# One matmul for the rows of B and C of both scan directions

## The chip, the cores and the metric

The kernel runs on one core of a Trainium2 chip, as one launch. The metric is device time in microseconds; before the change the median of three runs is 13519.48 us (13518.94 to 13551.32). Everything is float32.

## The reference

Eight images of 64 channels and 64 x 64 pixels go through four layers: an attention over all pixels, a block of windowed attention with an MLP, a dynamic filter, and a selective-scan layer. Only the last one is touched. With `x_flat` the pixels row by row and `x_t` column by column, it scans each image along four directions: both orders forwards (k = 0 and 1), and both backwards (k = 2 and 3).

```python
x_hwwh = jnp.stack([x_flat, x_t], axis=1)
xs = jnp.concatenate([x_hwwh, jnp.flip(x_hwwh, axis=-1)], axis=1)
x_dbl = jnp.einsum('bkdl,kcd->bkcl', xs, xproj_w)
dts, Bs, Cs = jnp.split(x_dbl, [R, R + N], axis=2)
dts = jnp.einsum('bkrl,kdr->bkdl', dts, dtproj_w)
dts = jax.nn.softplus(dts + dtproj_b[None, :, :, None])
A = -jnp.exp(A_logs).reshape(K, DI, N)
out_y = _selective_scan(xs, dts, A, Bs, Cs, Ds.reshape(K, DI))
...
def step(h, inp):
    u_t, dt_t, B_t, C_t = inp
    h = h * jnp.exp(dt_t[..., None] * A) + dt_t[..., None] * B_t[:, :, None, :] * u_t[..., None]
    return (h, jnp.einsum('bkcn,bkn->bkc', h, C_t))
```

There are DI = 128 channels and N = 16 states; R = 4 is the rank of dt. For every pixel and direction, B and C are 16 numbers each, made from the 128 channels of x at that pixel with weights of the direction's own. Directions k and k + 2 read the same pixels with different weights.

## The kernel before

The images are taken in four pairs (p = 0 to 3). What a pair needs before its scans is `front`, what follows them is `back`. While pair p is scanned, `scans` runs `back(p - 1)` and `front(p + 1)` beside it: these are generators that yield costs, and after each scan step as many of their pieces are written as the share of steps done allows. The scans of the last pair have only `back(2)` beside them, and `back(3)` comes after.

A *unit* is one chunk of TD = 512 pixels of one image in one direction. A pair has 64 units, in the order of directions k = 1, 3, 0, 2 for each image (`nth` counts them), 8 chunks each; k = 1 and 0 take the chunks from 0 to 7, k = 3 and 2 from 7 to 0. In the whole kernel there are 256 units, which this document numbers from 0 to 255: units 0 to 7 are k = 1, 8 to 15 are k = 3, 16 to 23 are k = 0, 24 to 31 are k = 2, and so on; 64, 128 and 192 begin the next pairs.

`inputs` prepares a unit: it loads `xs` (L1697), makes dt from it (matmul `pdd` L1700, exp L1702 and ln L1705 on ACT, dt times x in `du` L1706 on DVE, a copy of dt in `du` L1707 on ACT), then the 32 rows of B and C (matmul `pbc` L1709, copy `bc` L1711 on ACT) and writes the rows to memory (`rows`, L1713). It is called after step 1 of the unit before.

A unit has 8 *steps*, of two states each. `fetch` (L1720) loads the two rows of B, or of C, from `rows` and spreads them over all 128 partitions, 512 KB each time; B three steps ahead and C two steps ahead of use, with three buffers each. `products` (L1725) multiplies B with dt times x on POOL, two steps ahead. `step` takes exp of dt times A on ACT into a PSUM bank (`dad`, L1747; three banks with the tag `da`, which `pdd` and `pbc` also use), scans on DVE (L1750), keeps the last value in `carry` (L1758, ACT), and multiplies with C on POOL or DVE (L1761, L1765, L1770). `sums` adds up the states with matmuls into `yd` (L1789), and after a unit's last step adds the result to `Y` on DVE. For k = 2, the last direction, the sum goes into the unit's `xs` (L1804) and from there to memory (`ys`, L1805). `xs` has two buffers, `du` two, `rows` two.

For k = 1 and k = 2, `xs` is needed until the end of its unit, so its buffer is free for the unit after next only then; for k = 3 and k = 0 it is free as soon as the inputs are made.

The order in which instructions stand on each engine is made by a scheduler when the program is built: it takes the ready instruction that was written first, with a timing model of its own, and so may pull later-written instructions forward while others wait. SP issues all loads and stores of the scans from one queue, in a fixed order; an issue that waits holds those behind it.

Of the kernel before, what the change touches and what calls it, by code (L numbers as in the profile page):

```python
# [9 lines left out]
F32 = mybir.dt.float32  # L10
AF = mybir.ActivationFunctionType
# [12 lines left out]
DI, NST, RNK, KDIR = 128, 16, 4, 4  # L24
TD = 512
NTD = L // TD
# [62 lines left out]
def _pack(w):  # L89
    items = []  # L90

    def put(name, a):
        a = np.asarray(a, np.float32)
        shape = a.shape
        flat = a.reshape(shape[0], -1)
        if shape[0] < P:
            flat = np.concatenate([flat, np.zeros((P - shape[0], flat.shape[1]), np.float32)], axis=0)
        items.append((name, shape, flat))
# [91 lines left out]
    put("cb", _col(f["conv_b"]))  # L190
    xp = f["xproj_w"]
    put("xpT", np.concatenate([xp[:, RNK:], xp[:, :RNK]], axis=1).transpose(2, 0, 1))
    put("xbc", xp[:, RNK:].transpose(2, 0, 1))
    put("xr", xp[:, :RNK].transpose(1, 0, 2))
    put("drT", f["dtproj_w"].transpose(2, 0, 1))
    put("alogs", f["A_logs"].reshape(KDIR, DI, NST).transpose(1, 0, 2))
# [961 lines left out]
class _Direct:  # L1158
# [498 lines left out]
    def scans(self, p, beside, cost):  # L1657

        self.units = []
        for im in range(2):
            out = self.memory("ys")
            self.kept["y", 2 * p + im] = out
            for nth, k in enumerate((1, 3, 0, 2)):
                order = range(NTD) if k < 2 else range(NTD - 1, -1, -1)
                self.units += [dict(image=2 * p + im, k=k, c=c, at=at, nth=nth, out=out) for at, c in enumerate(order)]
        self.inputs(self.units[0])
        n = 8 * len(self.units)
        steps = [{} for _ in range(n)]  # L1670
        done = 0
        for i in range(-3, n):
            if i + 3 < n:
                self.fetch(i + 3, steps[i + 3], 0)
            if 0 <= i + 2 < n:
                self.fetch(i + 2, steps[i + 2], 1)
                self.products(i + 2, steps[i + 2])
            if i >= 0:
                self.step(i, steps[i])
                if i:  # L1680
                    self.sums(i - 1, steps[i - 1], steps[i]["w"])
                if p == B // 2 - 1 and done >= cost:
                    self.turn = max(self.turn, 0)
                while done < cost * (i + 1) / (n - LEAD):
                    done += next(beside, cost)
            if i % 8 == 1 and i // 8 + 1 < len(self.units):
                self.inputs(self.units[i // 8 + 1])
        self.sums(n - 1, steps[n - 1])
        self.run(beside)

    def inputs(self, u):

        nc, w, net = self.nc, self.w, self.net
        wk, ps = self.sw, self.ps
        k, c = u["k"], u["c"]
        x = u["x"] = wk.tile([P, TD], F32, name="xs", tag="xs")
        nc.sync.dma_start(x, self.kept[u["image"]][k % 2][:, c * TD : (c + 1) * TD])  # L1697

        pd = ps.tile([P, TD], F32, name="pdd", tag="da")
        nc.tensor.matmul(pd, lhsT=net.xdt[:, k, :], rhs=x, start=True, stop=True)  # L1700
        du = u["du"] = wk.tile([P, 2, TD], F32, name="du", tag="du")
        nc.scalar.activation(  # L1702
            pd, pd, AF.Exp, bias=w["dtb"][:, k : k + 1], accum_out=net.esum[:, u["image"], k, c : c + 1]
        )
        nc.scalar.activation(pd, pd, AF.Ln, bias=1.0)  # L1705
        nc.vector.tensor_tensor(du[:, 1], pd, x, ALU.mult)  # L1706
        nc.scalar.activation(du[:, 0], pd, AF.Copy)  # L1707
        pb = ps.tile([2 * NST, TD], F32, name="pbc", tag="da")
        nc.tensor.matmul(pb, lhsT=w["xbc"][:, k, :], rhs=x, start=True, stop=True)  # L1709
        bc = wk.tile([2 * NST, TD], F32, name="bc", tag="bc")  # L1710
        nc.scalar.activation(bc, pb, AF.Copy)  # L1711
        rows = u["rows"] = self.dram.tile([2 * NST, TD], F32, name="rows", tag="rows")
        nc.sync.dma_start(rows, bc)  # L1713

    def fetch(self, i, st, s):

# [245 lines left out]
```

## Time and profile before

| What | Value |
|---|---|
| median of 3 runs | 13519.48 us |
| the profiled execution | 13549.57 us |
| its span | 13547.6 us |
| mean granted TensorE clock | 0.882 |
| copy `bc` (L1711, ACT), 256 | median 586 ns |
| matmul `pbc` (L1709), 512 instructions for 256 | median 617 ns |
| weight load `pbc` (L1709), 512 | median 109 ns |
| matmul `pdd` (L1700), 512 instructions for 256 | median 668 ns |
| exp, ln, copy of dt (L1702, L1705, L1707; ACT) | median 662, 582, 577 ns |
| dt times x (L1706, DVE) | median 690 ns |
| product with B (L1725, POOL), 2048 | mean 2367 ns |
| scan (L1750, DVE) | mean 1270 ns |
| `B<-rows`, `C<-rows`, issue to landing | median 5.2, 4.6 us |
| `xs<-xt`, `xs<-xc`, issue to landing | median 3.5, 4.2 us |

A float32 matmul shows as two instructions. Durations of matmuls are modelled and overlap their neighbours, so what one takes of the engine is less than its duration when they follow each other closely. In the lines of waits the time is that in which the named engine, or SP's queue, stood before this line; what it stood for is the operation that came last. In timelines the columns are start, length (us), engine, line, operation, what it writes and reads, and the number merged.

### The profile page before, as it was taken

How to read it: one execution, taken by the hardware profiler on the slowest of the kernel's cores; microseconds unless marked ns; L12 is line 12 of the kernel's file. 1: busy time of each engine (PE TensorE's matmuls, PEld its weight loads, DVE VectorE, ACT ScalarE, POOL GpSimd, SP SyncE). 2: the span in 40 equal slices, each digit the busy share in tenths (PEclk: the TensorE clock that was granted, in tenths of full speed). 3: DMA queues.
4: the chain of work that ended last, by engine and by line, in shares of the span. 5: the costliest groups of instructions: out<-in, count | busy, mean ns of one | idle time of the engine just before them, and what ended most of it. 6: DMA issues, size and time to landing. Idle time of an engine off the chain costs nothing. (4 is left out here: it accounts for less than half of the span.)

```text
span 13547.6 us, 140341 instructions
## 1 busy us (share of the span) xinstructions
PE 10802.4 (80%) x45762; PEld 3981.2 (29%) x45762; DVE 8783.4 (65%) x10407; ACT 7087.6 (52%) x15569; POOL 7764.9 (57%) x3875
## 2 busy tenths in 40 slices
PE   9999986888787669989888667997898666666665
PEld 2243322333232222224432222223443222222221
DVE  0121236776668676676666767667675768988985
ACT  5556514564545646655554545665653644544542
POOL 0000004887778764466666685446675687777881
PEclk9999977998898779999889788998888788888887
DMA  0000004776667765455555674455554677787882
GB/s 24 1 1 1 3 13 170 238 238 211 207 218 244 235 200 168 155 186 175 169 178 175 221 250 168 158 167 176 186 192 151 209 241 262 235 280 264 303 283 86
DMA packets 706249, 2385.12 MB, mean 176 GB/s; under 512 B 81120, under 2 KB 81248, under 8 KB 704480
## 3 DMA queue, kind: packets, MB, share of 16 engines
q1 hardware_dynamic: 681312, 2319.76, 50.9%
q10 hardware_dynamic: 24192, 56.29, 1.1%
q8 instruction: 362, 5.93, 0.2%
q14 instruction: 383, 3.14, 0.1%
HBM read 2272.97 MB, written 102.76 MB: 175 GB/s over the span
## 5 line engine op out<-in xcount | busy, mean ns | idle before, releaser
L1725 POOL TENSOR_TENSOR vd<-B,du 128x1024 f32<-128x1024 f32 x2048 | 4832.8, 2367 | 3924.8 <-DMA B<-rows 2573.0
L1789 PE MATMUL yd<-vd,pack 128*128 128x512 f32 x7540 | 4263.8, 696 | 1381.0 <-POOL vd L1761 591.9
L1747 ACT ACTIVATE dad<-du,As 128x512 f32<-128x512 f32 x4096 | 2729.0, 681 | 1130.8 <-DVE hd L1750 684.1
L1750 DVE TENSOR_TENSOR_SCAN hd<-dad,carry,vd 128x512 f32<-128x512 f32 x2166 | 2713.2, 1270 | 677.8 <-ACT dad L1747 385.9
L1789 PEld LDWEIGHTS yd<-vd,pack 128*128 128x128 f32 x7540 | 1497.0, 215 | 3843.5 <-issue 1654.4
L1761 POOL TENSOR_TENSOR vd<-hd,C 128x1024 f32<-128x1024 f32 x658 | 1551.4, 2358 | 1068.2 <-DVE hd L1750 702.0
L1750 DVE TENSOR_TENSOR_SCAN dad<-dad,carry,vd 128x512 f32<-128x512 f32 x1418 | 1793.3, 1274 | 160.3 <-POOL vd L1725 99.1
L1765 POOL TENSOR_TENSOR vd<-hd,C 128x512 f32<-128x512 f32 x1154 | 1476.1, 1280 | 512.5 <-DVE hd L1750 446.4
L1313 ACT ACTIVATE e<-s 128x512 f32<-128x512 f32 x2048 | 1200.7, 591 | 751.1 <-PE s L1307 749.6
L1307 PE MATMUL s<-X 64*128 64x512 f32 x4096 | 1344.4, 646 | 30.5 <-ACT e L1313 28.8
L1299 PE MATMUL po<-e,VT 128*64 128x512 f32 x4096 | 1226.7, 621 | 12.6 <-ACT e L1313 9.9
L1765 DVE TENSOR_TENSOR vd<-dad,C 128x512 f32<-128x512 f32 x1300 | 864.9, 672 | 48.2 <-ACT carry L1758 39.1
L1758 ACT ACTIVATE carry<-hd 128x1 f32<-128x1 f32 (+1 forms) x1586 | 317.3, 201 | 920.3 <-DVE hd L1750 917.0
L1758 ACT ACTIVATE carry<-dad 128x1 f32<-128x1 f32 x1422 | 240.9, 169 | 804.1 <-DVE dad L1750 801.4
L1307 PEld LDWEIGHTS s<-X 64*128 64x128 f32 x4096 | 375.9, 186 | 915.2 <-issue 783.1
L1447 DVE TENSOR_TENSOR w_e<-w_s,bias 128x512 f32<-128x512 f32 x512 | 329.9, 681 | 424.3 <-PE w_s L1435 423.6
L1462 PEld LDWEIGHTS w_av<-vals,w_e 64*64 64x64 f32 x16384 | 546.7, 144 | 197.3 <-issue 86.8
L1462 PE MATMUL w_av<-vals,w_e 64*64 64x9 f32 x16384 | 574.9, 207 | 30.4 <-ACT w_e L1452 30.1
L1700 PE MATMUL pdd<-xs,xdt 128*128 128x512 f32 x512 | 348.3, 768 | 257.8 <-DMA xs<-xc 121.4
L1452 ACT ACTIVATE w_e<-w_e 128x512 f32<-128x512 f32 x512 | 311.8, 626 | 366.9 <-DVE w_e L1447 251.6
L1299 PEld LDWEIGHTS po<-e,VT 128*64 128x64 f32 x4096 | 236.1, 135 | 847.5 <-issue 763.9
L1574 PE MATMUL acc<-tap,pack 128*128 128x512 f32 x576 | 367.5, 761 | 99.5 <-DVE tap L1573 98.1
(252 smaller groups left out, 11129.2 us busy)
## 6 DMA issues: line engine op xcount, KB each, us to landing
B<-rows SPq DMA_DIRECT2D x2048, 512.0 KB, 5.2
C<-rows SPq DMA_DIRECT2D x2048, 512.0 KB, 4.6
xs<-xt SPq DMA_DIRECT2D x128, 256.0 KB, 3.5
xs<-xc SPq DMA_DIRECT2D x128, 256.0 KB, 4.2
xc<-xcv ACTq DMA_DIRECT2D x64, 256.0 KB, 4.0
zs<-z ACTq DMA_DIRECT2D x64, 256.0 KB, 3.7
xt<-XT ACTq DMA_DIRECT2D x32, 512.0 KB, 7.8
rows<-bc SPq DMA_DIRECT2D x256, 64.0 KB, 1.6
```

What stands on the lines that cost most here:

```text
L1299: nc.tensor.matmul(po[half[im]], lhsT=VT[:, t, half[im]], rhs=es[im], start=(t == 0), stop=(t == 31))
L1307: nc.tensor.matmul(ss[im], lhsT=at(half[im], t), rhs=X[half[im], jc * CH : (jc + 1) * CH], start=True, stop=True)
L1313: nc.scalar.activation(e, ss[im], AF.Exp, scale=C**-0.5, accum_out=parts[:, im, t, jc : jc + 1])
L1462: nc.tensor.matmul(self.av[half[im], x % 4 + j, h, :], lhsT=es[h // 4][half[im], j, h % 4, :], rhs=V[half[im], x + j, h, :], start=True, s ...
L1574: nc.tensor.matmul(acc, lhsT=w["ident"], rhs=tap, start=(t == 0), stop=(t == TAPS - 1))
L1725: self.nc.gpsimd.tensor_tensor(v, st["B"], dx.to_broadcast([P, 2, TD]), ALU.mult)
L1747: nc.scalar.activation(da, u["du"][:, 0], AF.Exp, scale=net.As[:, k, n : n + 1])
L1750: nc.vector.tensor_tensor_scan(along(to), along(da), along(v[:, j]), first, ALU.mult, ALU.add)
L1758: nc.scalar.activation(cs, ends, AF.Copy)
L1761: st["w"] = nc.gpsimd.tensor_tensor(v, h, CC, ALU.mult)
L1765: m = engine.tensor_tensor(v[:, j], hs[j], CC[:, j], ALU.mult)
L1789: m = nc.tensor.matmul(u["y"], lhsT=w["ident"], rhs=v, start=start, stop=stop)
```

## The change

For k = 1 and k = 0, the way out, one matmul now makes 64 rows: B and C of this direction and of the one that comes back over the same pixels. The weights `xbc` are reordered to 0, 2, 1, 3 so that the two directions' columns lie beside each other. The copy and the write are of 64 rows, and the tile in memory is kept in `rows_of` by chunk, with ten buffers (NTD + 2) for two. For k = 3 and k = 2, the way back, there is no matmul `pbc`, no copy `bc` and no write; `fetch` reads the second half of the rows that the way out wrote for the same chunk. `fetch`, `products`, `step` and `sums` are unchanged.

```diff
-    put("xbc", xp[:, RNK:].transpose(2, 0, 1))
+    put("xbc", xp[[0, 2, 1, 3], RNK:].transpose(2, 0, 1))
...
+        self.rows_of = {}
         self.inputs(self.units[0])
...
         nc.scalar.activation(du[:, 0], pd, AF.Copy)
-        pb = ps.tile([2 * NST, TD], F32, name="pbc", tag="da")
-        nc.tensor.matmul(pb, lhsT=w["xbc"][:, k, :], rhs=x, start=True, stop=True)
-        bc = wk.tile([2 * NST, TD], F32, name="bc", tag="bc")
-        nc.scalar.activation(bc, pb, AF.Copy)
-        rows = u["rows"] = self.dram.tile([2 * NST, TD], F32, name="rows", tag="rows")
-        nc.sync.dma_start(rows, bc)
+
+        nr = 2 * NST
+        if k < 2:
+            pb = ps.tile([2 * nr, TD], F32, name="pbc", tag="da")
+            both = w["xbc"][:, 2 * k : 2 * k + 2, :].rearrange("p a b -> p (a b)")
+            nc.tensor.matmul(pb, lhsT=both, rhs=x, start=True, stop=True)
+            bc = wk.tile([2 * nr, TD], F32, name="bc", tag="bc")
+            nc.scalar.activation(bc, pb, AF.Copy)
+            rows = self.rows_of[c] = self.dram.tile([2 * nr, TD], F32, name="rows", tag="rows", bufs=NTD + 2)
+            nc.sync.dma_start(rows, bc)
+        u["rows"] = self.rows_of[c][nr * (k // 2) : nr * (k // 2) + nr]
```

## The prediction

> **What bounds the kernel now.** The page comes first. Its chain of waits is too finely split to carry anything here (it spreads over dozens of lines at 0% each), so I went on to the groups, then to the waits of the engines and of SP's DMA queue, then to single units in the timeline.
>
> ```profile
> span 13547.6 us, 140341 instructions
> PE 10802.4 (80%) x45762; PEld 3981.2 (29%) x45762; DVE 8783.4 (65%) x10407; ACT 7087.6 (52%) x15569; POOL 7764.9 (57%) x3875
> PE   9999986888787669989888667997898666666665
> POOL 0000004887778764466666685446675687777881
> rows<-bc SPq DMA_DIRECT2D x256, 64.0 KB, 1.6
> ```
>
> No engine is full: PE is near full in some slices, POOL in others. The scans run from 2191 us (first product) to about 13285 us: 256 units in 11094 us, 43.3 us each, and the limit differs by stage. A table of busy time by stretch shows it:
>
> ```profile
> 5206.00:5591.00 385.00, 375.05 (x1148) 97.53 (x1146) 248.02 (x291) 260.20 (x781) 166.71 (x84) 0.99 0.49 159
> 12559.00:12787.00 228.00, 158.23 (x288) 53.57 (x288) 212.94 (x224) 118.07 (x280) 207.40 (x112) 0.90 0.88 306
> 12787.00:13019.00 232.00, 158.53 (x291) 53.46 (x290) 211.40 (x227) 117.55 (x281) 208.24 (x114) 0.90 0.88 302
> 13019.00:13256.00 237.00, 146.34 (x254) 47.44 (x254) 185.46 (x197) 106.32 (x259) 182.80 (x99) 0.86 0.75 265
> ```
>
> The columns after the length are PE, PEld, DVE, ACT, POOL. In the first row (attention beside the scans) PE is busy 97%. The last three are scans alone at the end: k=3 (8 units, 28.5 us each), k=0 (8 units, 29.0), k=2 (only 7 units from first product to first product, 33.9 each). DVE and POOL are over 90% in k=3 and k=0, but 78% in k=2: there a wait costs 5 us a unit. SP's own waits and the engines' name it:
>
> ```profile
> SPq L1713 <- ACT bc L1711: 1352.5, 209, 22.5
> SPq L1720 <- DMA rows<-bc: 142.4, 99, 4.8
> POOL vd L1725 <- DMA B<-rows: 2573.0, 255, 2174.4
> ACT pdd L1702 <- PE pdd L1700: 485.6, 155, 12.3
> DVE du L1706 <- ACT pdd L1705: 381.8, 155, 13.8
> ```
>
> (Columns: us in total, times, longest.) SP stands 1352 us before L1713 until `bc` is there, and every B and C fetch behind it stands too. POOL's 2573 us for B are 2174 us of the front before the scans, so 399 us remain. The other wait is the chain xs, pdd, exp, ln, du: 486 us on ACT. One k=2 unit in SP's timeline:
>
> ```profile
> 13126.79 0.32 SPq L1697 DMA_DIRECT2D xs<-xc  x1
> ...
> 13140.31 0.42 SPq L1713 DMA_DIRECT2D rows<-bc  x1
> 13144.15 0.32 SPq L1720 DMA_DIRECT2D C<-rows  x1
> 13144.58 0.37 SPq L1720 DMA_DIRECT2D B<-rows  x1
> 13146.74 0.32 SPq L1720 DMA_DIRECT2D C<-rows  x1
> ```
>
> xs leaves at 13126.8, after the store of the unit two back has freed its buffer; du is ready at 13139.7 (L1706); rows leave at 13140.3, land 3.4 us later, the unit's first B leaves at 13144.6 and lands at 13149.4, and POOL's first product starts at 13149.6: 10 us after du.
>
> **What the Trainium skill says.** "DMA: Bandwidth & Descriptors", section "Two DMAs through the same engine are not ordered": a DMA that reads what another wrote needs a wait for that one's completion. The trace agrees: B leaves only after rows have landed, 1.6 us after their issue at the median. "Perfetto Trace Analysis", section "Tensor Engine Instruction": ACT, DVE and GpSimd are strict FIFOs. The trace agrees: ACT stands 8.66 us before the exp of pdd at 7801 us while DVE idles for want of the `dad` behind it.
>
> **The change, part by part.** Units of k=3 and k=2 (128 of 256) lose a matmul, a copy and a DMA. The others make 64 rows where they made 32.
>
> *Wider rows, 128 units.* Nothing: the matmul still streams 512 columns, and the copy works on as many elements a partition. The write has 128 KB for 64; it lands in 1.6 us now, bounded by 0 and 1.6 us more, hidden in nearly all of these units by the other B in hand. I take 0.
>
> *Removed work.* 128 copies of 586 ns (L1711) are 75 us of ACT. 128 matmuls are two instructions each; in a run of eight `yd` matmuls an instruction takes 0.45 us, so 0.9 us each and 115 us of PE. Only where PE bounds is this on the path: 16 units (72 to 79, 136 to 143) at 97%, 16 x 0.9 = 14 us. A PSUM bank of the three of `da` is also free earlier.
>
> *Removed gate.* B and C of the way back no longer hang on bc and rows. Their source has been in memory for at least one unit, and ten buffers mean that the reuse waits for readers two units back or more: no new wait.
>
> - Scans alone at the end. k=2: 33.9 to about 29, the k=0 pace, 7 x 4.9 = 34 us. k=3: three units of eight (those from 234, 237 to the next and into 240) are gated today, 31 us against 26.7; they gain at most 12, I take 6. Together 40. Next late is du: xs issue to du is 12.9 us, some four steps of 3.4 us, and its product is five steps on.
> - Units 216 to 223 (34.2 us). POOL's first product is at B's landing there too, but DVE is dense from du to the unit's end; the loss is ACT's 7 us before exp (12169 to 12176). The changed program's instruction order puts exp half a step to a step and a half later (after the `dad` of five steps ahead rather than six), so ACT can go on while xs travels. Between 0 and 7 us; I take 3: 24 us.
> - Units 121 to 127 and 185 to 191 (37.8 us with POOL 87% busy, so 33 at least). Same wait, 6 to 9 us on ACT; exp moves by one and a half steps. Between 0 and 4.5 us, I take 2: 28. But three column blocks of `back` that fill these gaps in each of the two pairs are now ordered into the next pair, six blocks at about 2 us of DVE: minus 12. Net 16.
> - The remaining 74 units of the way back: PE mostly 82 to 90% busy, or POOL 89%. Between 0 and 1.5 us (one matmul and one copy, 0.9 + 0.6, both on the path); I take 0.6: 44.
>
> *Moved.* xs of k=3 was often pulled 5 or 13 fetches ahead while SP stood before rows; without that idle time it is issued in its written place, three fetches before its unit. In the first and last pair this touches 5 units in 8, 15 in all. I take 0, since exp moves back too; it is the basis of the slower rival. Two more activation table loads appear, 1.28 us each: 2.6, dropped.
>
> Sum: 14 + 40 + 24 + 16 + 44 = 138 us, taken as 140. The profiled execution took 13549.57 us, 30 above the median of 13519.48; the saving doesn't depend on that, so from the median: 13380 us.
>
> **Rivals.**
> 1. *The gate was cover.* Behind rows stands the du chain, which starts with the same xs; it takes the whole stall, and only PE's 14 us, 20 us at the end and a few more count: 13485. For it: ACT's 486 us before exp is more than POOL's 399 us for B. Against: in the k=2 unit above du is 10 us early.
> 2. *All units of the way back run at the pace of the dense ones.* 60 at the end, 56 in 216 to 223, 50 in the 14 units, 14 for PE, 80 for the rest: 260, so 13260. For it: SP's 1352 us of standing; half of it goes. Against: most first products come several us after B's landing.
> 3. *The loads come too late (slower).* xs is no longer pulled ahead, ACT meets the exp of pdd before xs has landed, and k=3 units of the first and last pair get the 7 us stall that k=2 has: 15 x 7 = 105 us, plus 30 for `back` work pushed into pairs bound by PE and DVE; against it 14 + 44 saved, nothing else: +77, 13597. It decides from 2 us of new wait a unit on, if the gains at the gate fail as well. For it: the same load in the same place stalls k=1 and k=2 today. Against: exp is ordered later.
>
> The row order is no rival: k and k+2 read the same xs, and the weights are reordered to match.
>
> **How the numbers follow.** Forecast 0.50, rival 1 0.21, rival 2 0.19, rival 3 0.10. Time 13380. Low end 13220 (rival 2 with the full bounds of the 74 units), high end 13530 (all gate terms nil), which leaves out rival 3 and a little of the tails. The forecast's own range is 13310 to 13450. Since 0.3% is 40 us, about what a measurement can tell: faster below 13479: 0.50 + 0.19 + a third of rival 1 = 0.76; slower 0.09; same 0.15.
>
> **What would show it.** 128 `bc` and `rows` in place of 256; SP's wait before rows near half of 1352 us; the last k=2 units at about 29 us with the first product some 2 us after du at the earliest, instead of 10; ACT's wait before pdd in 216 to 223 and 185 to 191 down from 7 us to 4; units 72 to 79 shorter by 0.9 us. It is wrong if k=3 units of the last pair exceed 28.5 us, if ACT's wait for pdd grows above 486 us in total, or if the later pairs' first units (128 on, 192 on) swell by more than the blocks moved there.

## The result, and the profile after

The changed kernel takes 13445.57 us (median of 6 runs, 13429.94 to 13482.82), beside 13528.71 us for the kernel before (6 runs, 13518.94 to 13551.32). The ratio is 0.9942, 95% interval 0.9928 to 0.9956: about 78 us less, where 140 were forecast. The predicted 13380 was too low by 66 us; the direction was right and the time lies in the range. The two profiled executions are 120 us apart where the medians are 83 apart, so the sum of the differences by stretch below is larger than the change itself.

The page, in the lines that answer to those of before:

```profile
span 13428.1 us, 139476 instructions
PE 10659.8 (79%) x45506; PEld 3995.1 (30%) x45506; DVE 8799.5 (66%) x10407; ACT 7009.7 (52%) x15443; POOL 7764.1 (58%) x3875
rows<-bc SPq DMA_DIRECT2D x128, 128.0 KB, 2.3
```

PE lost 143 us of work and ACT 78, with 256 and 126 instructions fewer. DVE and POOL are as busy as they were, within 20 us. The write of rows is twice as large and lands in 2.3 us where it took 1.6.

The waits of SP's queue (us in total, times, longest):

```profile
SPq L1718 <- ACT pdd L1706: 538.4, 59, 22.8
SPq L1718 <- ACT bc L1716: 161.8, 42, 11.6
```

L1718 is now the write of rows. The two together are 700 us, half of the 1352 before, as it must be with half of the writes. The engines' waits:

```profile
POOL vd L1731 <- DMA B<-rows: 434.1, 217, 14.0
ACT pdd L1703 <- PE pdd L1701: 420.1, 132, 15.2
DVE du L1707 <- ACT pdd L1706: 179.3, 100, 9.0
```

POOL waits for B no less than before (399 us there without the front). ACT's wait for pdd fell by 65 us, DVE's for du by 202. So what eased is the chain xs, pdd, exp, ln, du, and not POOL's wait for B. By stretches (length, then busy time of PE, PEld, DVE, ACT and POOL), after:

```profile
5122.31:5557.78 435.47, 423.64 (x1316) 109.69 (x1312) 281.08 (x335) 293.59 (x879) 190.42 (x96) 1.00 0.49 160
7888.50:8289.60 401.10, 276.11 (x546) 102.09 (x546) 312.71 (x347) 196.43 (x374) 262.01 (x124) 0.82 0.59 198
10766.18:11056.07 289.89, 177.02 (x298) 63.84 (x298) 195.51 (x185) 115.23 (x254) 264.70 (x131) 0.82 0.73 251
12443.31:12683.60 240.29, 156.35 (x273) 55.41 (x274) 216.44 (x226) 114.94 (x273) 207.49 (x114) 0.86 0.83 288
12911.55:13138.07 226.52, 141.24 (x238) 49.01 (x238) 186.10 (x197) 101.58 (x250) 181.51 (x100) 0.83 0.79 274
```

and before, for the two of these stretches that were not shown yet:

```profile
7988.30:8367.50 379.20, 246.44 (x498) 91.57 (x497) 299.86 (x329) 176.27 (x342) 263.47 (x124) 0.81 0.59 200
10864.84:11180.38 315.54, 205.19 (x368) 69.50 (x368) 212.22 (x204) 140.17 (x296) 266.92 (x132) 0.88 0.72 244
```

Units 72 to 79 lost 6.5 us (442.0 before, from first product to first product). Units 184 to 191 lost 25.6 us, but units 128 to 135 take 22 us more, with 18 more instructions and 13 us more work on DVE: part of this is work that moved over from the units ahead. The last two rows are where the forecast had its largest term. Units 232 to 239 (k=3) grew from 228.3 to 240.3 us, and the last k=2 units fell only from 236.5 to 226.5, to 32.4 us each and not 29. The whole last pair (units 192 to 255, to the end of the span) gained nothing, 2372 us for 2367; the saving lies in the three pairs ahead of it.

In those k=3 units the load of xs stands in another place. SP before, around units 234 to 236:

```profile
12608.79 0.42 SPq L1713 DMA_DIRECT2D rows<-bc  x1
12609.26 0.89 SPq L1697 DMA_DIRECT2D xs<-xt  x2
```

and after, two units in a row:

```profile
12540.73 0.42 SPq L1698 DMA_DIRECT2D xs<-xt  x1
...
12570.59 0.42 SPq L1698 DMA_DIRECT2D xs<-xt  x1
```

Before, two loads of xs leave at once, right behind rows. They are 36 and 62 us ahead of the first products of their units; after, each is 22 us ahead of its own, and nearly every unit takes 29.5 to 30.2 us. Before, a unit took 26.4 to 27.6 us where the xs of the next one had come early, and 30.4 to 31.7 where it had not.

A late k=2 unit (253) after, on SP and then on POOL:

```profile
13051.65 0.32 SPq L1698 DMA_DIRECT2D xs<-xc  x1
...
13063.62 0.38 SPq L1726 DMA_DIRECT2D B<-rows  x1
```

```profile
13068.30 2.37 POOL L1731 TENSOR_TENSOR vd<-B,du 128x1024 f32<-128x1024 f32 x1
13070.61 1.27 POOL L1771 TENSOR_TENSOR vd<-hd,C 128x512 f32<-128x512 f32 x1
13071.89 2.36 POOL L1731 TENSOR_TENSOR vd<-B,du 128x1024 f32<-128x1024 f32 x1
```

B of the unit leaves at 13063.6, with du (ready at 13063.8) and no longer 5 us behind it; the gate is gone. The first product (the last line) still comes 8 us after du, because POOL is busy until then with the unit before. What still takes the time is the chain that opens the unit: xs leaves 12 us before du is ready.

### The profile page after: what moved, and what is told of

The parts are those of the page before. It is cut to its first block, busy times and chain, and to the rows that moved or that the text cites. A ratio compares the mean times of both kernels' runs of the same rounds, so it can differ in the third digit from the quotient of the medians.

```text
span 13428.1 us, 139476 instructions
## 1 busy us (share of the span) xinstructions
PE 10659.8 (79%) x45506; PEld 3995.1 (30%) x45506; DVE 8799.5 (66%) x10407; ACT 7009.7 (52%) x15443; POOL 7764.1 (58%) x3875
## 5 line engine op out<-in xcount | busy, mean ns | idle before, releaser
L1307 PE MATMUL s<-X 64*128 64x512 f32 x4096 | 1358.3, 643 | 31.5 <-ACT e L1313 30.4
L1756 DVE TENSOR_TENSOR_SCAN hd<-dad,vd 128x512 f32<-128x512 f32 x304 | 363.4, 1211 | 138.0 <-ACT dad L1753 68.7
```

The lines of the kernel that those rows point to most:

```text
L1307: nc.tensor.matmul(ss[im], lhsT=at(half[im], t), rhs=X[half[im], jc * CH : (jc + 1) * CH], start=True, stop=True)
L1756: nc.vector.tensor_tensor_scan(along(to), along(da), along(v[:, j]), first, ALU.mult, ALU.add)
```

## The experiments

Each was timed beside runs of the kernel before (medians 13537 to 13541 us there), so the ratio is what is compared; 0.1% is 13.5 us. The last two columns are the time from a unit's first product on POOL to the next unit's, summed over the units of the way out (k=1, 0) and the way back (k=3, 2, to the end of the span). They come from one profiled execution each, so differences of some 10 us in them tell nothing.

| kernel | median us | ratio to before, 95% | way out | way back |
| --- | --- | --- | --- | --- |
| before | 13528.71 | 1 | 5469 | 5887 |
| changed | 13445.57 | 0.9942 (0.9928 to 0.9956) | 5516 | 5731 |
| e1_gate_only | 13690.02 | 1.0116 (1.01 to 1.0133) | 5538 | 5967 |
| e2_wide_only | 13547.74 | 1.0004 (0.9995 to 1.0013) | 5469 | 5896 |
| e3_before_pinned | 13724.18 | 1.0149 (1.013 to 1.0168) | 5548 | 5967 |
| e4_after_early2 | 13384.31 | 0.9888 (0.9871 to 0.9905) | 5513 | 5676 |
| e5_work_only | 13699.49 | 1.0119 (1.0099 to 1.0138) | 5499 | 6006 |
| e6_write_only | 13468.24 | 0.9953 (0.9937 to 0.9969) | 5530 | 5739 |
| e7_after_early3 | 13090.62 | 0.9681 (0.966 to 0.9701) | 5306 | 5600 |
| e8_before_early2 | 13473.02 | 0.9947 (0.993 to 0.9964) | 5446 | 5831 |
| e9_bank_only | 13584.74 | 1.0036 (1.0023 to 1.005) | 5522 | 5866 |
| e10_time_only | 13547.87 | 1.0000 (0.9991 to 1.0008) | 5524 | 5837 |
| e11_before_early3 | 13217.79 | 0.9774 (0.9761 to 0.9787) | 5315 | 5710 |
| e12_order_only | 13586.57 | 1.0033 (1.002 to 1.0047) | 5537 | 5876 |

The diffs are against the changed kernel, but for e3, e8 and e11, which start from the kernel before, and e2 and e9, which are shown against e1 and e5.

### Gate or work: e1, e5, e6, e2

First the work of the way back was put back without its gate.

```diff
@@ inputs, e1_gate_only @@
             nc.sync.dma_start(rows, bc)
+        else:
+            pb = ps.tile([nr, TD], F32, name="pbc", tag="da")
+            nc.tensor.matmul(pb, lhsT=w["xbc"][:, 2 * (k - 2) + 1, :], rhs=x, start=True, stop=True)
+            bc = wk.tile([nr, TD], F32, name="bc", tag="bc")
+            nc.scalar.activation(bc, pb, AF.Copy)
+            spare = self.dram.tile([nr, TD], F32, name="spare", tag="spare")
+            nc.sync.dma_start(spare, bc)
```

> The changed kernel, but units of the way back (k=2, 3) still do their own matmul, copy and row write, into a tile that nothing reads; their B and C come from the rows of the way out, as in the changed kernel. So the work is back and the gate is gone. Theory G (the saving comes from the gate: SP no longer lets B and C of the way back wait for bc): most of the 83 us stay, 13445 to 13480, and units 72 to 79 return to 442 us. Rival W (the saving comes from the removed matmuls and copies): 13510 to 13535.

1.0116. Neither theory had it: not only is the saving gone, the kernel is 157 us slower than before, and 235 slower than the changed one. But SP still stands before the write to `spare`, so this run had SP's wait as well as the work. The next two separate them. e5_work_only is e1 without its last two lines; e6_write_only keeps only the write:

```diff
@@ inputs, e6_write_only @@
             nc.sync.dma_start(rows, bc)
+        else:
+            spare = self.dram.tile([nr, TD], F32, name="spare", tag="spare")
+            nc.sync.dma_start(spare, du[0:nr, 0])
```

> The changed kernel with the matmul and the copy to bc put back in units of the way back, but without a row write: nobody reads bc, so SP has nothing to wait for. Only PE's and ACT's work is back. The run with work and row write (e1_gate_only) took 13690. Theory S (what costs there is SP standing before the write, with every fetch behind it): this one stays near the changed kernel, 13460 to 13530, at most 128 x 1.5 us above it if all the work lay on the path, and most of that less. Rival W (the work itself, in the way of exp and ln): 13600 or more.

> The changed kernel with a row write put back on SP in units of the way back, without the matmul and the copy: 64 KB of du, as soon as ACT's copy into du is done, into a tile that nothing reads. Only SP's wait for the du chain and the write are back. Theory S: most of the 245 us between e1_gate_only and the changed kernel, 13570 to 13680. Rival W: 13440 to 13490.

e5 gives 1.0119, e6 0.9953. Theory S falls: SP's standing and the write cost 0.11% in e6, some 15 us, inside the intervals, and nothing beside the work (e1 against e5). The work alone costs 1.77%, 239 us, or 1.9 us for each of the 128 units, all of it in the way back (6006 against 5731). The trace of the kernel before says that nearly this much is there to save, if all of it lies on the path. Its rows for `pbc` (busy us, mean ns of one):

```profile
L1709 PE MATMUL pbc<-xs,pack 128*32 128x512 f32 x512 | 318.0, 708 | 16.8 <-DVE hd L1750 16.7
L1711 ACT ACTIVATE bc<-pbc 32x512 f32<-32x512 f32 x256 | 148.5, 580 | 106.1 <-PE pbc L1709 104.9 <-DMA B<-rows 0.6
```

Two instructions of 0.71 and a copy of 0.58 are 2.0 us a unit. That these durations are where the time goes isn't shown by the sum, though, as the runs of the next group show.

```diff
@@ inputs, e2_wide_only: as e1_gate_only, but @@
-        u["rows"] = self.rows_of[c][nr * (k // 2) : nr * (k // 2) + nr]
+        u["rows"] = self.rows_of[c][0:nr] if k < 2 else spare
```

> The kernel before, except that units of the way out write 64 rows where they wrote 32 (ten row buffers), the upper half read by nobody; the way back makes and reads its own 32 rows. Only the wider rows are added. Theory: they cost nothing, as the prediction took it: 13529 within 20 us. Rival: the longer write holds back the first B of units of the way out, up to 1.6 us in 128 units but mostly hidden: 13560 or more.

In e2 the units of the way out make 64 rows in ten buffers and the way back keeps its own 32. 1.0004: the wider rows cost nothing that can be seen, as the prediction took them.

e2 shows more than that. It has the same instructions as e1, and differs from it in this one line: in e2 the way back reads the rows that it has just written, so its B and C have the gate; in e1 it doesn't. e1 is 1.12% slower, 152 us. Taking the gate away with all the work kept, and with it the instruction order that was built around it, lost more on balance than the whole change saves. The queue of SP shows why in part. A k=3 unit in e2 and then in e1:

```profile
12623.78 0.42 SPq L1725 DMA_DIRECT2D spare<-bc  x1
12624.26 0.94 SPq L1698 DMA_DIRECT2D xs<-xt  x2
12627.64 0.32 SPq L1733 DMA_DIRECT2D C<-spare  x1
```

```profile
12753.08 0.42 SPq L1725 DMA_DIRECT2D spare<-bc  x1
12753.59 0.37 SPq L1733 DMA_DIRECT2D B<-rows  x1
12756.92 2.91 SPq L1733 DMA_DIRECT2D C<-rows  x2
```

Both stand before the same write. In e2 the fetches behind it must wait until it has landed, and in that gap the program's order has two loads of xs; in e1 a fetch can follow at once, and xs stays in its late place. Of the 64 loads of xs for k=3, 50 stand more than three B fetches ahead of their unit in the kernel before and in e2, 37 in e1 and 35 in the changed kernel. Units 232 to 239, where nothing but scans runs, go from 228.8 us in e2 to 259.1 in e1. That is not all of the 152 us: units 208 to 223 take 67 us more in e1, 19 of which units 200 to 207 give back, and DVE's work moves with it, so pieces of `back` stand elsewhere too. How the 152 us divide between late loads and moved pieces was not separated.

### What makes the work dear: e9, e10, e12

The work occupies PE and ACT, and it takes one of the three PSUM banks that pdd and dad share. It also changes the order: in e5 the exp of pdd stands a half to one and a half steps earlier in ACT's queue than in the changed kernel, in most units of the way back. Three runs take these apart.

```diff
@@ inputs, e9_bank_only: as e5_work_only, but @@
-            nc.tensor.matmul(pb, lhsT=w["xbc"][:, 2 * (k - 2) + 1, :], rhs=x, start=True, stop=True)
+            few = pb[:, 0:64]
+            nc.tensor.matmul(few, lhsT=w["xbc"][:, 2 * (k - 2) + 1, :], rhs=x[:, 0:64], start=True, stop=True)
             bc = wk.tile([nr, TD], F32, name="bc", tag="bc")
-            nc.scalar.activation(bc, pb, AF.Copy)
+            nc.scalar.activation(bc[:, 0:64], few, AF.Copy)
@@ inputs, e10_time_only @@
         nc.tensor.matmul(pd, lhsT=net.xdt[:, k, :], rhs=x, start=True, stop=True)
+        if k >= 2:
+            nc.tensor.matmul(pd, lhsT=net.xdt[:, k, :], rhs=x, start=True, stop=True)
...
+        else:
+            bc = wk.tile([nr, TD], F32, name="bc", tag="bc")
+            nc.scalar.activation(bc, x[0:nr], AF.Copy)
@@ step, e12_order_only (the exp of pdd is kept as u["exp"]) @@
-            nc.scalar.activation(da, u["du"][:, 0], AF.Exp, scale=net.As[:, k, n : n + 1])
+            m = nc.scalar.activation(da, u["du"][:, 0], AF.Exp, scale=net.As[:, k, n : n + 1])
+            soon = self.units[i // 8 + 1] if i // 8 + 1 < len(self.units) else {}
+            if soon.get("k", 0) >= 2 and 2 * (i % 8) + j == (6 if soon["image"] == B - 1 else 5):
+                net.behind(m, soon["exp"])
```

> As e5_work_only, but the matmul and the copy put back in units of the way back cover 64 of the 512 columns, so that they take little of PE and ACT; they still take one of the three PSUM banks that pdd and dad share, between the two, and the exp of pdd stands in ACT's order where it does in e5_work_only (a half to one and a half steps earlier than in the changed kernel). Theory B (the cost is the bank and the order of exp against dad on ACT): 13630 to 13710, like e5_work_only. Theory D (the cost is the duration, 1.4 us of PE and 0.6 us of ACT in the chain from xs to du): 13470 to 13540.

> The changed kernel; in units of the way back the matmul of pdd is done twice into the same bank, and ACT copies 32 rows of xs to bc, which nobody reads. The durations of the removed matmul and copy are back (a little more on PE), no bank is, and exp stands a half step later in ACT's order than in the changed kernel. Theory B: 13440 to 13540. Theory D: 13630 to 13710.

> The changed kernel with no work put back; on ACT alone, the exp of pdd of each unit of the way back is ordered ahead of the dad before which it stands in e9_bank_only (a half to one and a half steps earlier than in the changed kernel). It separates the two that e9_bank_only (13585, ratio 1.0036 to before) has together: the place of exp in ACT's queue, and the PSUM bank. Theory O (ACT, first in first out, stands before exp for xs while dad waits behind it): most of the 127 us between e9_bank_only and the changed kernel, 13530 to 13590. Theory K (the bank: the scan has one dad fewer while pbc holds it): 13440 to 13490.

e9 comes out between its two theories (1.0036, 0.94% above the changed kernel), e10 as well (1.0000, 0.58% above). Together 1.52% of e5's 1.77%: a bit more than half of the work's cost is in what e9 keeps, the rest in the durations. e10 is the weaker of the two, since its second matmul stands ahead of exp, where that of e5 stands behind, and exp itself moves later. e12, which adds no instruction, gives 1.0033, the same as e9 within the intervals. So e9's part is the place of exp in ACT's queue, and no cost of the bank beyond moving exp there can be seen. Theory K falls. e12 also gives the durations a second time: from e5 to e12 the matmul and the copy go and exp stays early (in some 40 units one `dad` later than in e9), and that is 0.86%, 116 us; from e12 to the changed kernel only the order changes, and that is 0.91%, 123 us.

Unit 188 (k=2) shows how. In the kernel before, ACT and then DVE:

```profile
10997.34 0.66 ACT L1702 ACTIVATE pdd<-pdd,pack 128x512 f32<-128x512 f32 x1 [8.44 <-PE pdd L1700]
...
10998.76 0.69 DVE L1706 TENSOR_TENSOR du<-pdd,xs 128x512 f32<-128x512 f32 x1 [8.41 <-ACT pdd L1705]
10999.54 0.67 ACT L1747 ACTIVATE dad<-du,As 128x512 f32<-128x512 f32 x1
```

ACT stands 8.4 us before the exp of pdd, whose xs has not landed; the `dad` that the scans want is queued behind it, and DVE stands too. In the changed kernel:

```profile
10882.84 0.69 ACT L1753 ACTIVATE dad<-du,As 128x512 f32<-128x512 f32 x1 [1.57 <-DVE hd L1756]
...
10884.12 0.67 ACT L1753 ACTIVATE dad<-du,As 128x512 f32<-128x512 f32 x1
10885.05 1.28 DVE L1756 TENSOR_TENSOR_SCAN hd<-dad,carry,vd 128x512 f32<-128x512 f32 x1 [1.07 <-POOL vd L1731]
10886.25 1.27 DVE L1756 TENSOR_TENSOR_SCAN dad<-dad,carry,vd 128x512 f32<-128x512 f32 x1
...
10888.95 0.66 ACT L1703 ACTIVATE pdd<-pdd,pack 128x512 f32<-128x512 f32 x1 [4.15 <-PE pdd L1701]
```

Three more `dad` go ahead of exp (two of them in these lines), two scans run while xs travels, and the wait is 4.15 us. (Not all of it is won: behind these two scans DVE waits 5.45 us for POOL.) In e12, where exp alone is put early again:

```profile
10984.04 0.66 ACT L1703 ACTIVATE pdd<-pdd,pack 128x512 f32<-128x512 f32 x1 [9.99 <-PE pdd L1701]
10984.72 0.68 ACT L1753 ACTIVATE dad<-du,As 128x512 f32<-128x512 f32 x1
...
10985.43 1.28 DVE L1759 TENSOR_TENSOR_SCAN hd<-dad,carry,vd 128x512 f32<-128x512 f32 x1 [8.42 <-ACT dad L1753]
```

ACT waits 9.99 us, DVE 8.42 for the `dad` behind, and units 184 to 191 take 311.0 us again in place of 289.9. The Trainium skill ("Perfetto Trace Analysis", section "Tensor Engine Instruction") calls ACT a strict FIFO; these lines agree, and e12 puts a price on it. Unit 188 is one of the clearer ones: ACT's waits for pdd in all of units 184 to 191 are 41.4 us before, 36.3 in the changed kernel and 68.8 in e12.

### The place of xs: e3, e4, e8

```diff
@@ inputs and fetch, e3_before_pinned @@
-        nc.sync.dma_start(x, self.kept[u["image"]][k % 2][:, c * TD : (c + 1) * TD])
+        load = nc.sync.dma_start(x, self.kept[u["image"]][k % 2][:, c * TD : (c + 1) * TD])
+        if self.last_b is not None:
+            net.behind(load, self.last_b)
...
+        if s == 0:
+            self.last_b = m
@@ scans, e4_after_early2 and e8_before_early2 (load() issues xs; inputs() only if it hasn't been) @@
                 self.inputs(self.units[i // 8 + 1])
+                if i // 8 + 2 < len(self.units) and self.units[i // 8]["k"] in (3, 0):
+                    self.load(self.units[i // 8 + 2])
```

> The kernel before, with each xs load ordered on SP's queue behind the B fetch that is written ahead of it, so that it can't be pulled ahead while SP stands before rows. Theory P (the changed kernel gives back part of its saving because xs of k=3 is no longer pulled ahead): slower than before by 40 to 60 us, 13570 to 13590, with units 232 to 239 at 240 us or more instead of 228. Rival N (the place of xs does not matter): 13520 to 13540, units 232 to 239 at 226 to 230.

> The changed kernel; the load of xs for the second unit after one of k=3 or k=0 is issued at that unit's second step, where its buffer is already free, so about eleven B fetches ahead of its unit instead of three. Nothing else is changed. Theory P: 30 to 60 us faster than the changed kernel, 13385 to 13415, units 232 to 239 back at 228 us or less. Rival N: 13430 to 13460, units 232 to 239 at about 240.

> The kernel before with the same edit as e4_after_early2 (early xs after units of k=3 and k=0). Theory P says that before got most of this by itself, from SP's standing before rows in k=3, but not in k=0 and in the gated units: 13460 to 13520, so that the change is worth 75 to 135 us with xs in the same early place, against 279 us with xs in the same late place (e3_before_pinned against the changed kernel). Rival (the early xs and the sharing of rows do the same thing): 13390 to 13430, so that the change is worth nothing once xs is early.

Theory P has the direction in all three. Without the pulling ahead, the kernel before is 1.49% slower, far more than expected. Of the 157 us between the two profiled executions, 80 lie in the way back (72 in k=3), where the change takes the early loads away, and about as many in k=0, where it doesn't. So e3 takes away more than the change does: no load stands early in e3, and the changed kernel keeps 35 of 64 in k=3 and 56 of 64 in k=0, as many there as before. Units 232 to 239 take 257.1 us in e3, 32 each. With xs early after k=3 and k=0, the changed kernel gains 0.54%, and units 232 to 239 come to

```profile
12444.63:12662.07 217.44, 150.40 (x274) 53.65 (x274) 211.32 (x225) 114.16 (x273) 207.67 (x114) 0.90 0.91 321
```

27.2 us each, with DVE 97% and POOL 96% busy: the stall is gone and DVE and POOL are nearly full. The rival of e8 falls too: the kernel before gains 0.53% by the same edit, and the change is still worth 0.59% on top of it.

e1 and e3 also give the gate its own price, where they can be compared. Both do all the work of the way back; e3 has the gate at rows, e1 hasn't. In units 232 to 239 every xs stands three fetches ahead in both, and they take 257.1 us with the gate and 259.1 without: once xs is late, the gate itself costs nothing there. (The whole way back is 5967 us in both by accident: e1 is 52 us shorter in k=3 and 52 longer in k=2, and its loads are not all late.)

### A version faster than both: e7, e11

```diff
@@ scans, e7_after_early3 and e11_before_early3 (load() with three xs buffers, bufs=3; bc with bufs=1) @@
+        self.load(self.units[0])
+        self.load(self.units[1])
         self.inputs(self.units[0])
...
                 self.inputs(self.units[i // 8 + 1])
+                if i // 8 + 2 < len(self.units):
+                    self.load(self.units[i // 8 + 2])
```

> The changed kernel with three xs buffers in place of two (paid for by one bc buffer in place of two), and every xs issued one unit earlier, at the second step of the unit before the last one. The variant with two buffers, early only where the buffer was free, took 13384. Theory P (a late xs is what stalls a unit): the k=1 and k=2 units gain too, 13270 to 13350, with the last k=2 units at 29 us or less in place of 32 to 33. Rival: the rest is bound by DVE and POOL, 13370 to 13400.

> The kernel before with the same edit as e7_after_early3: three xs buffers, every xs a unit earlier, one bc buffer. If the work in the way back costs only because a late xs puts the opening of each unit on the path, it is hidden here, except in the 16 units where PE is full and in the wait for bc and rows: 13110 to 13180, within 100 us of e7_after_early3 (13091). If it costs 2 us a unit wherever it stands: 13330 or more.

e7 is the fastest of all: 13090.62 us, 0.9681. It was expected at 13270 to 13350; the early loads help the way out as well, by 210 us, nearly all of it in k=1. The last units of k=3 and k=2 are

```profile
12152.28:12363.87 211.59, 150.68 (x274) 53.74 (x274) 211.16 (x225) 113.82 (x273) 207.53 (x114) 0.90 0.95 328
12579.67:12785.27 205.60, 134.56 (x238) 48.76 (x238) 184.00 (x197) 100.86 (x250) 181.46 (x99) 0.88 0.86 303
```

so 26.4 us each with DVE at 99.8%, and 29.4 each. e11 missed its expectation: 13218, 0.93% above e7 where within 100 us was expected. So the work of the way back, with the gate and the order that come with it, isn't fully hidden once xs is early; it costs about 1 us a unit still, half of what the work costs with a late xs. In the last units of k=3 and of k=2 it is hidden: they take 214.6 and 205.6 us in e11, 211.6 and 205.6 in e7. Of the 110 us by which the way back of e11 is longer, 68 lie in units 88 to 95, 104 to 111, 152 to 159 and 168 to 175 of the two middle pairs; why there was not tried.

## Why the prediction was right, and which of its steps were wrong

**The total was near by luck: two large errors had opposite signs.** Five steps lead from the kernel before to the changed one (each ratio is sure to some 0.1 to 0.2%):

| from, to | what changes | ratio | us |
| --- | --- | --- | --- |
| before, e2 | wider rows on the way out | +0.04% | 5, inside the interval |
| e2, e1 | the gate goes | +1.12% | 152 |
| e1, e5 | the write of the way back goes | +0.03% | 4, inside the interval |
| e5, e12 | matmul and copy go, exp stays early | -0.86% | -116 |
| e12, changed | exp moves later on ACT | -0.91% | -123 |

The prediction had about 110 us for the last two together (14 + 44 + 24 + 28) where the runs give 239, and for the second step it had a gain of 40 less 12 where the runs give a loss of 152. Its terms one by one:

- *Removed work.* The prediction put 14 us on PE where it is full and 44 on 74 other units, at 0.6 us of a possible 1.5. This was too small: durations are 78 us (e10) to 116 (e5 to e12). The matmul was priced at 0.9 us from a run of `yd`; its own row in the profile gives 2 x 0.71, and PE's busy time fell by 1.1 us for each. The 0.9 us a unit where PE is full look exact (6.5 us in units 72 to 79, 6.4 in 136 to 143), but are no evidence for the price. e12 has none of the matmuls back and takes 443 us again in units 72 to 79. Before, and then e12 (the changed kernel is shown above, with 1.00 as granted clock):

```profile
5158.70:5600.69 441.99, 429.93 (x1320) 111.72 (x1318) 282.41 (x332) 297.28 (x884) 190.50 (x97) 0.99 0.49 159
5174.84:5617.85 443.01, 429.45 (x1308) 110.94 (x1308) 281.32 (x333) 293.54 (x877) 190.17 (x96) 0.98 0.47 156
```

The granted clock there is 0.99, 1.00 and 0.98 in the three, so part of the 6.5 us may be the clock of the one execution; how much is open.

- *exp later in ACT's order.* The step saw the mechanism, and its size where it was counted: 24 + 28 us in 22 units, where e12 is 49 us longer than the changed kernel in units 120 to 127, 184 to 191 and 216 to 223. But it was left out of the other units, and over the whole kernel it is 123 us, about half of what work and order save. The waits had been read too evenly: before, ACT's waits for pdd in units 121 to 127 and 185 to 191 go from nothing to 8.8 us, where 6 to 9 was read. In units 216 to 223 the wait fell as said, from 53.7 to 31.4 us in total, yet the stretch grew by 15 us: DVE is 88% busy there, for 75 before.
- *Removed gate, 40 us at the end.* This step failed. B does leave with du now, but nothing came of it: with the loads equally late the gate itself is worth nothing in units 232 to 239 (e3 and e1), and SP's standing with the write is 15 us in e6, inside the intervals. Rival 1, the gate as cover for the du chain, had that right. Its 13485 was too slow because it counted almost nothing for the order of exp.
- *xs no longer pulled ahead, taken as 0.* This step failed too, on the other side, and it belongs to the gate: the gap between the write of rows and the fetches that wait for it is where the early loads stood. The reason given for 0, that exp moves back too, was wrong for the last pair, where k=3 units rose to 30 us each; the text had named 28.5 as the mark above which it would be wrong. Rival 3 put this loss at 105 us, with 30 for pieces of `back` pushed into other places; the 135 are near the 152 of e1 against e2. It was wrong as a whole because it left only 58 us for what work and order save.
- *Blocks of `back` moved, minus 12.* Units 121 to 127 and 185 to 191, with the unit ahead of each, lost 45 us in all; units 128 to 135 and 192 to 199 take 32 more. The net of 13 is near the forecast's 16, but both sides were larger than said (45 for 28, and 32 for 12). A larger move was not foreseen: in the last pair units 200 to 207 lost 43 us, and units 208 to 215 and 216 to 223 take 31 and 15 more, with 46 and 49 us more of DVE. The way out as a whole takes 47 us more; it takes 69 more in e1 than in e2, so this comes with the gate's removal and not with the wider rows.
- *Wider rows, 0.* Held (e2): the matmul of 64 rows takes 0.71 us an instruction as that of 32 does, the copy 0.59 us for 0.58.

Of what the prediction said would show it, 128 rows, SP's wait at half, the shorter units 72 to 79 and the shorter wait before pdd in 216 to 223 came. The wait in 185 to 191 hardly fell (41.4 to 36.3 us with the unit ahead), and the k=2 units at 29 us with the first product 2 us after du did not come. ACT's wait for pdd in total fell from 486 to 420 and so did not give the warning that the last k=3 units gave.

## What to carry to other kernels

Before removing a wait, ask what the program's order has put into it: here the gap between a write and the fetches that wait for it was where later loads stood, and closing the gap put those loads back in their late place, which is part of a loss of 1.12%. On an engine that runs first in, first out, the place of an instruction that waits for a load can count as much as the durations of what is removed (0.91% beside 0.86% here); removing a small operation nearby can move it. When units open with a chain of load, matmul and activations, load one unit further ahead first: here that was worth four times the change.

## What the runs showed that was not expected

- Taking away a dependency and nothing else made the kernel 1.12% slower (e1 against e2).
- Ordering one activation a half to one and a half steps earlier in two of three units of the way back, with no work added, cost 0.91% of the kernel (e12 against the changed kernel).
- A matmul of 32 rows and a copy, 2.0 us in their own rows, cost 1.9 us a unit on engines that are 79% and 52% busy (e5), about half of it by the order that they bring.
- A third buffer of xs, with loads a unit earlier, took 2.6% off the changed kernel (0.9942 to 0.9681) and 2.3% off the one before, the largest effects of all runs.
